# Query, value and output products from split factors in the last six blocks, and expert weights fetched by chunk

## The chip, the cores and the metric

The kernel runs on one core of one Trainium2 chip. The metric is the device time of one execution in microseconds (us). Three runs of the kernel before gave 1141.47, 1142.01 and 1142.49 us; the median is 1142.01 us.

## What is computed

The reference is one transformer layer on 4096 tokens of 512 numbers (2 sequences of 2048), all in float32. Each half of the layer adds a normalised result to its input.

```python
x = x + layernorm(attention(layernorm(x)))
x = x + layernorm(experts(layernorm(x)))

# attention: 16 heads of 32, 64 latent keys, the 4 best of them per token and head
Q = h @ Wq.T + bq;  V = h @ Wv.T + bv          # 512 x 512 each
logits = einsum('bhtd,lhd->bhtl', Q, latent) / sqrt(32)
top, idx = top_k(logits, 4)
weighted = einsum('bhtk,bhtkd->bhtd', softmax(top), latent[idx])
out = (weighted + V) @ Wo.T + bo

# experts: weights rounded to -1, 0, 1 times one scale per matrix; 2048 hidden
hidden = silu(h @ Wu.T) * (h @ Wg.T)
out = hidden @ Wd.T
```

## The kernel before, in words

**Tiling.** The 4096 tokens are cut into 8 blocks of 512 (`NB = 8`, `TB = 512`), and a block into 4 tiles of 128 tokens (`TT = 4`). The 2048 hidden columns of the experts are cut into 16 chunks of 128 (`EC = 16`). The main loop (L1020) goes over blocks b and, inside, over chunks e. While the experts of block b run, the attention of block b+1 is worked in between, and the first normalisation of block b+2 too. A prologue (the list `FIRST_STEPS`) does the attention of block 0, the queries of block 1, and the rounding of the expert weights. So the loop of block 0 carries the attention of block 1 (without queries), the loops of blocks 1 to 6 carry the attentions of blocks 2 to 7 in full, and the loop of block 7 carries none.

**Order of work.** The order is written out by hand: each engine (TensorE, VectorE, ScalarE, GpSimd, and SyncE's queue, which issues all DMAs) takes its instructions in the order in which the Python code emits them. In a chunk e this order is:

```python
F.up("u", e); do(3); F.tanh(e); do(0); F.silu(e)
F.up("g", e); do(1); F.gate(e); F.high(e)
F.down(e - 1); do(2); F.low(e)
```

`do(k)` emits whatever `pieces` (L937) has put at place (e, k) by `put(e, k, f, ...)`: the steps of the attention. `up("u")` is 8 matmuls into the PSUM bank "u", `up("g")` 8 into the bank "g", `down(e - 1)` 8 into the four banks "acc". Each of the banks "u" and "g" is there once, so `up("u", e + 1)` waits until `silu(e)` on VectorE has read "u", and `up("g", e + 1)` until `gate(e)` on VectorE has read "g". `down(e)` needs `low(e)`, the last thing that VectorE does in chunk e. Two more banks, "at", are shared by all steps of the attention.

**Types.** Expert matmuls work on float32r operands, one pass each; the hidden numbers and the normalised input are given as a high and a low part (`hi`, `lo`; `hT_f`, `lT_f`), which makes two matmuls of each. The products of the attention (`q` L349, `v` L435, `y_pe` L455, `o` L464, `l` L361) are plain float32 matmuls; the trace shows each as two matmul instructions.

**Steps of the attention.** `q(c)` is a quarter of the queries, with its bias added on ScalarE; `l(c)` the logits of four heads, as two tiles w(2c), w(2c+1) that ScalarE copies out. For each of the eight tiles w(i): `m` (eight best), `r` (mark the four best, subtract the largest), `e` (exponentials on ScalarE), `n` (normalise), `z` (transpose and send through DRAM to a transposed tile wT). Tile i has `m` in chunk i+1, `r` in chunk i+1 at place 2, `e` in chunk i+2 at place 3, ahead of `tanh`, and `n` and `z` in chunk i+2. `v(c)` and `y_pe(c)` add V and the weighted latent vectors in one bank, `o(t)` is the output product of a tile of tokens, `o_bias` adds bo on VectorE. The normalisations, the residual sums on GpSimd and the transposes for the next experts (`f_blocks`, `f_load`, `f_split`, through DRAM) follow in chunks 11 to 15. `a_stats`, `a_apply`, `a_blocks` in chunks 9 and 10 prepare block b+2, and `a_load` brings its transposed input hT at the end of chunk 15. The result of the experts is normalised by `y_stats` (chunk 0 of the next block) and `y_out` (chunk 1), which frees the four "acc" banks.

**Memory.** All rounded expert weights stay on chip in 24 buffers of 128 x 1024 (tag "chunk"), wq, wv and wo in float32 beside them.

Of the kernel before, what the change touches and what calls it, by code (L numbers as in the profile page):

```python
# [17 lines left out]
P = 128  # L18
# [11 lines left out]
TAKEN = -3.2e38  # L30

# [15 lines left out]
"""  # L47

# [10 lines left out]
def latent_attention_ternary_glu(  # L59
# [43 lines left out]

    def acc_psum(name):
        return ps_acc.tile([P, D], F32, tag="acc", name=name)

    def transposed(which, b, name, dtype):  # L110
        return work.tile([P, DC, TB], dtype, tag=f"{which}{b % 2}", name=name, bufs=1)
# [10 lines left out]
    late = work.tile([P, DC, D], F32, tag="xa", name="raw_d_6", bufs=1)  # L122
    for n, i in RAW_ORDER:
        raw[n, i] = wpool.tile([P, CH], F32, tag="chunk", name=f"raw_{n}_{i}", bufs=6 * DC)
    for q in range(DC):
        raw["d", 6 + q] = late[:, q, :]
# [13 lines left out]
    def load_normed(b):  # L140
        normed[b] = work.tile([P, TT, D], F32, tag="xa", name=f"xa_{b}", bufs=1)
        nc.sync.dma_start(
            out=normed[b], in_=x_in[b * TB : (b + 1) * TB, :].rearrange("(t p) d -> p t d", p=P)
        )
# [9 lines left out]
    wq = wpool.tile([P, DC, D], F32, name="wq")  # L154
    wv = wpool.tile([P, DC, D], F32, name="wv")
    wo = wpool.tile([P, DC, D], F32, name="wo")
# [75 lines left out]
    def sign(n, i):  # L232
        j = i if n != "d" or i < 6 else 6 + (i - 6) // 2
        if (n, j) not in tern:
            tern[n, j] = wpool.tile([P, CH], F32R, tag="chunk", name=f"tern_{n}_{j}", bufs=6 * DC)
        q = tern[n, j] if j == i and i < 6 or n != "d" else tern[n, j][:, (i % 2) * D : (i % 2 + 1) * D]
        nc.scalar.activation(q, raw[n, i], AF.Sign, bias=minus_magic)

# [52 lines left out]
    class Attention:  # L291
# [15 lines left out]
        def a_stats(self, t):  # L307
            self.norm_a.stats(t, normed[self.b][:, t, :])
# [4 lines left out]
        def a_apply(self, t):  # L313
            self.norm_a.apply(normed[self.b][:, t, :], normed[self.b][:, t, :], t)
# [14 lines left out]
        def a_blocks(self, t):  # L329
            self.blocks("a", t, normed[self.b][:, t, :])  # L330

        def a_load(self):
            self.hT = transposed("X", self.b, f"hT_{self.b}", F32)
# [101 lines left out]
        def v(self, c, psum=at_psum):  # L435
            if self.attnT is None:
                self.attnT = transposed("Y", self.b, f"attnT_{self.b}", F32)
# [74 lines left out]
        def f_load(self, half):  # L512
            if half == 0:
                self.whole = work.tile([P, 4, TB], F32, tag="xa", name=f"hw_{self.b}", bufs=1)
# [7 lines left out]
        def f_split(self, t):  # L522
            if t == 0:
                self.hi = transposed("X", self.b, f"hT_f{self.b}", F32R)
                self.lo = transposed("Y", self.b, f"lT_f{self.b}", F32R)
# [11 lines left out]

    class FirstAttention(Attention):  # L540
# [19 lines left out]
        def a_trans_pe(self, t):  # L560
            if self.hT is None:
                self.hT = transposed("X", self.b, f"hT_{self.b}", F32)
# [53 lines left out]
        def v_pe(self, c):  # L616
            if self.attnT is None:
                self.attnT = transposed("Y", self.b, f"attnT_{self.b}", F32)
# [68 lines left out]
        def f_high(self, t):  # L687
            if not hasattr(self, "hi"):
                self.hi = transposed("X", self.b, f"hT_f{self.b}", F32R)
            nc.scalar.copy(self.hi[:, :, t * P : (t + 1) * P], self.pt[t])  # L690

        def f_low(self, t):
            if not hasattr(self, "lo"):
                self.lo = transposed("Y", self.b, f"lT_f{self.b}", F32R)
# [7 lines left out]
    class Experts:  # L702
# [6 lines left out]
        def up(self, n, e):  # L709
# [5 lines left out]
            for k, i in pairs:  # L715
                nc.tensor.matmul(  # L716
                    p, lhsT=tern[n, 2 * k + e // 8][:, (e % 8) * P : (e % 8 + 1) * P],
# [3 lines left out]


# [29 lines left out]
        def down(self, e, tiles=range(TT), last=True):  # L752
            if e == 0:
                self.acc = [acc_psum(f"acc_{self.b}_{t}") for t in range(TT)]
            wd = tern["d", e // 2][:, (e % 2) * D : (e % 2 + 1) * D]
# [46 lines left out]
        def y_out(self, t, engine=nc.gpsimd):  # L802
# [4 lines left out]
            else:  # L807
                y = row(f"y_{self.b}_{t}")
                self.norm.apply(y, self.acc[t], t)
# [29 lines left out]
    def query_place(c):  # L839
        if c < 3:  # L840
            if not hasattr(nxt, "early"):
                nxt.early = transposed("Y", 1, "qT_1", F32)
# [94 lines left out]
    def pieces(A, after):  # L937
# [6 lines left out]
        if A.b > 1:  # L944
# [12 lines left out]
        for c in range(2):  # L957
            if A.b > 1:
                put(4 + 2 * c, 0, A.v, c, gate_psum)
                put(4 + 2 * c, 0, A.y, c)  # L960
            put(4 + 2 * c, 0, A.l, c + 2)
            if A.b == 1:

                put(4 + 2 * c, 2 - c, A.v, c)
                put(4 + 2 * c, 2 - c, A.y, c)
        for c in range(2, DC):
            put(4 + 2 * c, 1, A.v, c)
            put(4 + 2 * c, 1, A.y, c)
# [15 lines left out]
        put(10, 2, A.o, 0, range(DC), gate_psum)  # L984
        put(10, 2, A.o_bias, 0)
        for t in range(1, TT):
# [4 lines left out]
            put(10, 2, A.o, t)  # L991
# [174 lines left out]
```

## Time and profile before

| what | value |
|---|---|
| profiled execution, span from first to last instruction | 1140.3 us |
| the three timed runs, median | 1142.01 us, 1.7 us above the span |
| TensorE busy | 1127.9 us of the span (99%), granted clock 0.998 |
| VectorE, ScalarE, GpSimd busy | 836.3, 411.9, 163.5 us |
| one middle block, 499.0 to 637.5 us | 138.5 us: TensorE 138.4, VectorE 104.7, ScalarE 43.5, GpSimd 17.3 us busy |
| DMA in the same stretch | 28% of 16 engines, 84 GB/s |

A matmul's own duration in the profile contains its way through the array; what counts for throughput is the distance between starts. "PE" is a matmul, "PEld" its load of weights, which overlaps other matmuls. "DVE" is VectorE, "ACT" ScalarE, "POOL" GpSimd, "SP" SyncE's queue. L716 is `up`, L759 `down`, L353 `q`, L440 `v`, L457 `y_pe`, L468 `o`, L367 `l`.

### The profile page before, as it was taken

To read this page: it belongs to the slowest core of one execution; us is meant where nothing else is said; L and a number is where in the kernel's file an instruction comes from. 1 tells how busy PE (TensorE), PEld (TensorE's weight loads), DVE (VectorE), ACT (ScalarE), POOL (GpSimd) and SP (SyncE) were. 2 spreads that over 40 slices of the span, in tenths; PEclk is the share of its full clock that TensorE was granted. 3 is DMA by queue.
4 is the path that set the end of the run, shared out by engine and by line. 5 is a ranking of instruction groups with operands and counts; after the bars stand their busy time and mean duration, and the time that the engine had idled before them with its cause. 6 is when DMAs were issued, how large, how long until landed. Compare 5 with 4: busy or idle time off the path is not lost.

```text
span 1140.3 us, 14487 instructions
## 1 busy us (share of the span) xinstructions
PE 1127.9 (99%) x4602; PEld 771.9 (68%) x4602; DVE 836.3 (73%) x2952; ACT 411.9 (36%) x714; POOL 163.5 (14%) x203
## 2 busy tenths in 40 slices
PE   9999999999999999999999999999999999999997
PEld 5547666767667675776657766586675866758886
DVE  6978968687866887678877778678786787847435
ACT  4985642332233332333214333153321433224223
POOL 1057003110032000320002200022001120021200
PEclk9999999999999999999999999999999999999999
DMA  9800221432213322222222222232321412102000
GB/s 350 305 0 20 74 93 38 111 120 84 82 52 98 102 86 81 72 77 93 93 74 75 83 93 95 63 99 66 112 75 56 111 65 93 61 5 74 37 1 37
DMA packets 98428, 97.16 MB, mean 85 GB/s; under 512 B 8368, under 2 KB 70832, under 8 KB 98352
## 3 DMA queue, kind: packets, MB, share of 16 engines
q1 hardware_dynamic: 98352, 96.24, 26.8%
q8 instruction: 36, 0.59, 0.2%
q14 instruction: 40, 0.33, 0.1%
HBM read 59.51 MB, written 36.70 MB: 84 GB/s over the span
## 4 chain that ended last, share of the span: by engine, by line
PE 89%; DVE 5%; DMA 4%; ACT 1%; issue 0%; SPq 0%; ACTq 0%; DVEq 0%
PE pg L716 20%; PE pu L716 19%; PE acc L759 19%; PE po L468 8%; PE pv L440 8%; PE pq L353 7%; PE pv L457 2%; PE pl L367 2%; DMA raw_d<-in_wdT 1%; DVE left L393 1%; DMA raw_g<-in_wgT 1%; DMA wv<-in_wvT 1%; DVE m L385 1%; DMA raw_u<-in_wuT 1%; PE pq L577 1%; DMA hT<-far_a 1%
## 5 line engine op out<-in xcount | busy, mean ns | idle before, releaser
L716 PE MATMUL pg<-hT_f,tern_g 128*128 128x512 f32 x512 | 207.8, 406 | 0.0
L716 PE MATMUL pu<-hT_f,tern_u 128*128 128x512 f32 x512 | 204.8, 401 | 0.0
L759 PE MATMUL acc<-tern_d,hi 128*128 128x512 f32 x512 | 203.6, 398 | 0.0
L759 PE MATMUL acc<-tern_d,lo 128*128 128x512 f32 x512 | 200.0, 391 | 1.0 <-DVE lo L749 0.9
L716 PE MATMUL pg<-lT_f,tern_g 128*128 128x512 f32 x512 | 199.8, 390 | 0.0
L716 PE MATMUL pu<-lT_f,tern_u 128*128 128x512 f32 x512 | 199.1, 390 | 0.0
L725 ACT ACTIVATE h<-pu,columns 128x512 f32<-128x512 f32 x128 | 87.1, 680 | 202.8 <-PE pu L716 202.8
L728 DVE SCALAR_TENSOR_TENSOR h<-h,pu 128x512 f32<-128x512 f32 x128 | 85.9, 671 | 93.5 <-ACT h L725 93.5
L744 ACT CAST hi<-h 128x512 fp32r<-128x512 f32 x128 | 79.1, 618 | 199.2 <-DVE h L733 199.1
L733 DVE TENSOR_TENSOR h<-h,pg 128x512 f32<-128x512 f32 x128 | 86.5, 675 | 63.4 <-PE pg L716 62.3
L759 PEld LDWEIGHTS acc<-tern_d,hi 128*128 128x128 f32 x512 | 96.2, 188 | 32.8 <-issue 13.6
L716 PEld LDWEIGHTS pg<-hT_f,tern_g 128*128 128x128 f32 x512 | 96.2, 188 | 25.3 <-issue 1.4
L716 PEld LDWEIGHTS pu<-hT_f,tern_u 128*128 128x128 f32 x512 | 96.1, 188 | 25.1 <-issue 3.1
L759 PEld LDWEIGHTS acc<-tern_d,lo 128*128 128x128 f32 x512 | 96.2, 188 | 22.9 <-DVE lo L749 2.2
L716 PEld LDWEIGHTS pu<-lT_f,tern_u 128*128 128x128 f32 x512 | 96.2, 188 | 22.5 <-issue 3.1
L716 PEld LDWEIGHTS pg<-lT_f,tern_g 128*128 128x128 f32 x512 | 96.3, 188 | 21.5 <-issue 2.9
L749 DVE TENSOR_TENSOR lo<-h,hi 128x512 fp32r<-128x512 f32 x128 | 89.9, 702 | 23.1 <-ACT hi L744 23.1
L440 PE MATMUL pv<-hT,wv 128*128 128x512 f32 x224 | 100.8, 593 | 0.3 <-ACT w L375 0.3
L393 DVE MATCH_REPLACE8 left<-m,w 128x64 f32<-128x64 f32 x512 | 100.3, 209 | 0.0
L468 PE MATMUL po<-wo,attnT 128*128 128x512 f32 x224 | 97.3, 592 | 0.0
L353 PE MATMUL pq<-hT,wq 128*128 128x512 f32 x192 | 86.7, 595 | 0.9 <-DMA hT<-far_a 0.6
L468 PEld LDWEIGHTS po<-wo,attnT 128*128 128x128 f32 x224 | 42.6, 190 | 50.7 <-issue 48.3
(140 smaller groups left out, 1312.0 us busy)
## 6 DMA issues: line engine op xcount, KB each, us to landing
dz<-z SPq DMA_DIRECT2D x56, 256.0 KB, 2.0
wT<-dz SPq DMA_DIRECT2D x224, 64.0 KB, 1.9
x<-in_x SPq DMA_DIRECT2D x32, 256.0 KB, 3.7
out_x<-x SPq DMA_DIRECT2D x32, 256.0 KB, 2.0
far_f<-zf SPq DMA_DIRECT2D x28, 256.0 KB, 2.8
hw<-far_f SPq DMA_DIRECT2D x56, 128.0 KB, 3.5
xa<-in_x SPq DMA_DIRECT2D x6, 1024.0 KB, 5.3
far_a<-za SPq DMA_DIRECT2D x24, 256.0 KB, 2.9
```

The costliest lines, as they stand in the source:

```text
L353: nc.tensor.matmul(pq, lhsT=wq[:, k, c * P : (c + 1) * P], rhs=self.taken(k), start=(k == 0), stop=(k == DC - 1),)
L367: nc.tensor.matmul(pls[pr][:, t * P : (t + 1) * P], lhsT=qT[rows, t * P : (t + 1) * P], rhs=lk[rows, c, :], start=True, stop=True, tile_po ...
L393: nc.vector.match_replace(left[:, g, :], m8[:, g, :], w[:, g, :], TAKEN)
L440: nc.tensor.matmul(self.pv[c], lhsT=wv[:, k, c * P : (c + 1) * P], rhs=self.ordered(k), start=(k == 0), stop=False,)
L468: nc.tensor.matmul(self.po[t], lhsT=self.attnT[:, c, t * P : (t + 1) * P], rhs=wo[:, c, :], start=(c == 0), stop=(c == DC - 1),)
L716: nc.tensor.matmul(p, lhsT=tern[n, 2 * k + e // 8][:, (e % 8) * P : (e % 8 + 1) * P], rhs=self.parts[i][:, k], start=(k, i) == pairs[0], s ...
L725: nc.scalar.activation(self.h[e], self.pu[e], AF.Tanh, scale=half_u[0])
L728: nc.vector.scalar_tensor_tensor(self.h[e], self.h[e], 1.0, self.pu.pop(e), ALU.add, ALU.mult)
L733: nc.vector.tensor_tensor(self.h[e], self.h[e], self.pg.pop(e), ALU.mult)
L744: nc.scalar.copy(hi, self.h[e])
L749: nc.vector.tensor_tensor(lo, self.h.pop(e), self.hid[e][0].bitcast(F32), ALU.subtract)
L759: nc.tensor.matmul(self.acc[t], lhsT=part[:, t * P : (t + 1) * P], rhs=wd, start=(e == 0 and i == 0), stop=(e == EC - 1 and i == 1),)
```

## The change

In the loops of blocks 1 to 6 (the attentions of blocks 2 to 7) the products q, v and o are no longer four-by-four float32 matmuls. Each factor is split into a high part (times `CUT`, rounded to float32r) and the rest, and from these a third, combined tile is formed. One product becomes three float32r matmuls: 4 into a "cross" bank and 8 into a "high" bank, and the two banks are joined by ScalarE (cross plus bias) and VectorE (high times 1 + 2^-12, plus that).

- `SplitAttention` replaces `Attention` for blocks 2 to 7. Its input is split by `x_high` (ScalarE), `x_low` and `x_difference` (VectorE), two instructions of 128 x 1024 each; `v_split` splits the sum of V and the weighted vectors (two on ScalarE, one on VectorE, one on GpSimd for each c). `a_load` moves from chunk 15 to chunk 12.
- A `q` or a `v` takes two banks: both "at" banks. `o` takes "u" and "g" for tiles 0 and 2, both "at" banks for tiles 1 and 3. The addition of bo moves from VectorE to GpSimd.
- `v` moves from chunks 4, 6, 8, 10 to chunks 5, 7, 8 and the end of 9.
- In `r` the subtraction of the largest from w leaves VectorE; a small instruction (`least`) takes its place, and `e` becomes eight exponentials of 64 columns with that as bias instead of one of 512.
- `y_out` applies the normalisation on ScalarE (`apply_scalar`) instead of VectorE.
- wq, wv and wo are split once (`parts`, in the loops of blocks 0 and 1) into 18 of the 24 "chunk" buffers. So the rounded expert weights are written to DRAM during block 0 (`keep`), and from block 1 on each chunk's weights are fetched two chunks ahead (`fetch_up`, 512 KB a chunk; `fetch_down`, 512 KB every second chunk), through SyncE's queue.

```diff
+    def part_high(n, w, j):
+        h = unit(f"{n}_high_{j}", F32R)
+        nc.scalar.activation(h, w[:, 2 * j : 2 * j + 2, :], AF.Copy, scale=CUT)
...
+    def part_rest(n, w, j):
...
+        nc.vector.tensor_tensor(src, src, h.bitcast(F32), ALU.subtract)
+        low = unit(f"{n}_low_{j}", F32R)
+        nc.scalar.activation(low, src, AF.Copy, scale=1.0 / STEP)
...
+    class SplitAttention(Attention):
...
+        def x_high(self, j):
...
+            nc.scalar.activation(
+                self.piece("h", j), self.piece("d", j).bitcast(F32), AF.Copy, scale=CUT
+            )
+        def x_low(self, j):
...
+            nc.vector.tensor_tensor(
+                self.piece("l", j), self.piece("d", j).bitcast(F32),
+                self.piece("h", j).bitcast(F32), ALU.subtract,
+            )
+        def x_difference(self, j):
+            nc.vector.scalar_tensor_tensor(
+                self.piece("d", j), self.piece("h", j).bitcast(F32), -STEP,
+                self.piece("l", j).bitcast(F32), ALU.mult, ALU.add,
+            )
...
+        def products(self, n, c, high, cross, moving):
+            cols = slice(c * P, (c + 1) * P)
+            for k in range(DC):
+                nc.tensor.matmul(
+                    cross, lhsT=form(n, "d", k)[:, cols], rhs=moving("d", k),
+                    start=(k == 0), stop=(k == DC - 1 and n == "q"),
+                )
+            for i, which in enumerate("hl"):
+                for k in range(DC):
+                    nc.tensor.matmul(
+                        high, lhsT=form(n, which, k)[:, cols], rhs=moving(which, k),
+                        start=(i == 0 and k == 0), stop=(i == 1 and k == DC - 1),
+                    )
+        def joined(self, dst, high, cross, bias):
+            nc.scalar.activation(dst, cross, AF.Identity, bias=bias)
+            nc.vector.scalar_tensor_tensor(dst, high, 1.0 + STEP, dst, ALU.mult, ALU.add)
...
+        def v_split(self, c):
...
+            nc.scalar.activation(h, self.sum, AF.Copy, scale=CUT)
+            nc.scalar.activation(d, self.sum, AF.Copy, scale=CUT * STEP)
+            nc.vector.tensor_tensor(l, self.sum, h.bitcast(F32), ALU.subtract)
+            nc.gpsimd.tensor_tensor(d, l.bitcast(F32), d.bitcast(F32), ALU.subtract)
+        def o(self, t, high, cross):
+            toks = slice(t * P, (t + 1) * P)
+            order = [("d", k) for k in range(DC)] + [(w, k) for w in "hl" for k in range(DC)]
+            if t == 0:
+                order = [(w, k) for w in "hld" for k in range(DC - 1)]
+                order += [(w, DC - 1) for w in "hld"]
...
+        def o_bias(self, t):
...
+            nc.scalar.copy(o, cross)
+            nc.gpsimd.tensor_tensor(o, o, bo_sb, ALU.add)
+            nc.vector.scalar_tensor_tensor(o, high, 1.0 + STEP, o, ALU.mult, ALU.add)
...
+        def e(self, i):
+            nc.scalar.activation(self.top[i], self.top[i], AF.Exp)
+            for g in range(G):
+                nc.scalar.activation(
+                    self.w[i][:, g, :], self.w[i][:, g, :], AF.Exp, bias=self.least[:, g, :]
+                )
...
-                self.norm.apply(y, self.acc[t], t)
+                self.norm.shift(t)
+                self.norm.apply_scalar(y, self.acc[t], t)
...
+        if split:
+            for c, e in enumerate((5, 7, 8)):
+                put(e, 1, A.v, c)
+                put(e, 1, A.y_pe, c)
+                put(e, 2, A.v_join, c)
+                put(e + 1, 0, A.v_split, c)
+            put(9, 2, A.v, 3)
+            put(10, 1, A.y_pe, 3)
+            put(10, 1, A.v_join, 3)
+            put(10, 1, A.v_split, 3)
...
+            put(12, 0, after.a_load)
+            late = after.b == 2
+            for j in range(2):
+                put(15 if late else 13, 2, after.x_high, j)
+            for j in range(2):
+                put(15 if late else 14, 2 if late else 0, after.x_low, j)
+            for j in range(2):
+                put(15, 2, after.x_difference, j)
...
+        i = b * EC + e + 2
+        if EC <= i < NB * EC:
+            fetch_up(i)
+        if e % 2 and EC <= i - 1 < NB * EC:
+            fetch_down(*divmod((i - 1) // 2, EC // 2))
+    def parts(b, e):
+        for n, w, at_b, at_e in (("q", wq, 0, 8), ("v", wv, 0, 11), ("o", wo, 1, 0)):
+            if b == at_b and 0 <= e - at_e < 2:
+                part_high(n, w, e - at_e)
+                part_rest(n, w, e - at_e)
+                part_difference(n, e - at_e)
```

## The prediction

> **What bounds the kernel now.** I read the page's busy table and chain first, then the chain in order of time for one middle block, then the timeline of all engines.
>
> ```profile
> PE 1127.9 (99%) x4602; PEld 771.9 (68%) x4602; DVE 836.3 (73%) x2952; ACT 411.9 (36%) x714; POOL 163.5 (14%) x203
> ...
> PE 89%; DVE 5%; DMA 4%; ACT 1%; issue 0%; SPq 0%; ACTq 0%; DVEq 0%
> ```
>
> TensorE has almost no gap, and the chain that ends last is TensorE for 89%. The chain in order of time (start, length) gives the price of each group:
>
> ```profile
> 504.75 3.44 PE pq L353 x8
> 508.18 1.82 PE acc L759 x8
> ...
> 558.75 1.81 PE pg L716 x8
> ...
> 588.03 13.73 PE po L468 x32
> ```
>
> A float32 instruction costs 0.43 us (3.44 / 8), a float32r one 0.227 (1.81 / 8). But VectorE is close behind. In the first block, where no q stands between the chunks, the timeline shows it as the bound already:
>
> ```profile
> 108.59 0.68 DVE L749 TENSOR_TENSOR lo<-h,hi 128x512 fp32r<-128x512 f32 x1
> ...
> 109.33 0.50 PE L759 MATMUL acc<-tern_d,lo 128*128 128x512 f32 x1 [0.41 <-DVE lo L749]
> ...
> 116.25 0.68 DVE L749 TENSOR_TENSOR lo<-h,hi 128x512 fp32r<-128x512 f32 x1
> ...
> 116.99 0.50 PE L759 MATMUL acc<-tern_d,lo 128*128 128x512 f32 x1 [0.45 <-DVE lo L749]
> ```
>
> From `lo` to `lo` VectorE needs 7.66 us a chunk there, and TensorE waits for it. What fills them shows in chunk 8 of a middle block:
>
> ```profile
> 565.72 0.18 DVE L397 TENSOR_TENSOR top<-m 128x32 f32<-128x32 f32 x1
> 565.82 0.68 DVE L749 TENSOR_TENSOR lo<-h,hi 128x512 fp32r<-128x512 f32 x1
> 566.00 0.23 ACT L402 ACTIVATE top<-top 128x32 f32<-128x32 f32 x1 [1.82 <-DVE top L397]
> 566.13 0.61 ACT L403 ACTIVATE w<-w 128x512 f32<-128x512 f32 x1
> 566.42 1.10 DVE L385 MAX8 m<-w 128x8 f32<-128x64 f32 x8
> 566.65 0.67 ACT L725 ACTIVATE h<-pu,columns 128x512 f32<-128x512 f32 x1
> ...
> 567.60 0.65 DVE L728 SCALAR_TENSOR_TENSOR h<-h,pu 128x512 f32<-128x512 f32 x1
> 568.17 0.18 DVE L408 TENSOR_REDUCE ri<-top 128x8 f32<-128x32 f32 x1
> ...
> 570.54 0.65 DVE L733 TENSOR_TENSOR h<-h,pg 128x512 f32<-128x512 f32 x1
> ```
>
> Call T the end of `lo` (566.50). The order is a loop through two engines: `r` ends, ScalarE does `e` and then `tanh` (ends T+0.82), VectorE does `m` (to T+1.10), `silu` (0.57), `n` and `z` (2.37), `gate` (0.57), the marks of `r` (1.67), its subtraction (0.60), `top` (0.11), `lo` (0.68): 7.67 in all. `lo` has slack before TensorE needs it: it ends at 510.70, and `down` begins at 514.79.
>
> **What the change removes.** Each (c, k) product goes from 2 x 0.43 to 3 x 0.227 us, 0.185 less. 48 products in a block make 8.9 us, six blocks 53 us. All of it is on the path, as long as nothing else sets it. The FP8 and Floating Point Precision page of the Trainium skill (TensorE Precision Notes) counts float32 as four passes; three of four would save a quarter, 10.4 us a block at 0.864 us a product, where the rows give 8.9; the rows decide.
>
> **What it adds, through one middle block** (t = 0 at the end of the last `down` of the block before; before: 495.53). I follow the emitted order with the rows' durations.
>
> *Chunks 0 and 1.* `q(0)` now has a join on VectorE, queued ahead of `y_stats`: it starts when the query ends (2.95) and `y_stats` run 3.6 to 6.8 instead of from about -1. GpSimd's rsqrt (2.07, 636.66 to 638.73) ends at 9.0. The four normalisations on ScalarE (spacing 0.71) end at 10.0 to 12.1; `down(0)` wants the four banks at 10.4 to 11.7 and waits 0.4. Behind them on ScalarE stands the bias of `q(1)` (to 12.75), behind that on VectorE its join (13.4), `m` (14.6), `gate` (15.2), `r`, `lo` (17.75). `down(1)` wants that `lo` at 17.5: the slack of 4.1 us is gone.
>
> *Chunks 2 to 8*, from `lo` to `lo`. Eight exponentials take the place of one: a row of 32 columns moves on after 0.13 us (566.00 to 566.13), and 32 columns more are 32 x 0.81 ns (0.615 for 512 against 0.227 for 32), so 0.16 to 0.17 each, 1.34 for eight where one cost 0.52. `tanh` ends at T+1.64, so `silu` starts at 1.67 and not 1.10. `least` (0.13, between the 0.09 of a memset and the 0.20 of a reciprocal) replaces the subtraction. A plain chunk: 1.67 + 0.57 + 2.37 + 0.57 + 1.67 + 0.13 + 0.11 + 0.68 = 7.8 (chunks 2, 4). With a query (3, 5) its bias waits on ScalarE for `tanh` (to 2.3), the join follows on VectorE (to 2.95), then `m`: 10.2, and 10.8 with the join of `v(0)` in 5. A split V (6, 8) puts ScalarE's split and VectorE's difference ahead of `silu`: 9.5 in 6 (two copies of w come first), 9.0 in 8 with a join, 8.4 in 7. Sum 63.5.
>
> *To chunk 10.* `z(7)` ends 5.2 after `lo(8)`; its way through DRAM is the next price (SyncE's timeline, and a line of the list of DMA issues with the time to landing):
>
> ```profile
> 578.20 0.34 SPq L425 DMA_DIRECT2D dz<-z  x1
> 580.28 1.73 SPq L428 DMA_DIRECT2D wT<-dz  x4
> ...
> wT<-dz SPq DMA_DIRECT2D x224, 64.0 KB, 1.9
> ```
>
> The last issue starts at 581.6 and lands 1.9 later: 5.4 us after `z`. Then `y_pe(3)` takes 1.15. So `down(9)` starts at 17.75 + 63.5 + 5.2 + 5.4 + 1.15 = 93.0. Before it was 90.4 (585.92), and TensorE alone would now be there at 84.1 (eight quarters of q and v less, 5.9, and the wait of 0.4 for hT gone): 8.9 of waits in place of 6.3 of gain.
>
> *Chunk 10.* `gate(10)` frees the bank "g" for `o(0)`, and VectorE reaches it only after the join and the difference of `v(3)` (2.95 after `down(9)` starts, because they need `y_pe(3)`) and four `a_apply` (1.92): 5.45, where `o(0)` wants it at 3.2. With 0.3 more for a bank, `o(3)` ends 15.05 after `down(9)` starts; before 15.5; without waits 12.7.
>
> *Chunk 11 to the next block.* 27.4 before. GpSimd's addition of bo (1.3 us) lies between ScalarE and VectorE in each `o`, `low(10)` comes 0.4 late; GpSimd's residual sums start 5.5 after `o(3)` instead of 3.8 (605.16 against 601.4), half of which chunk 12 takes up, so the transposed input of the experts comes 1 us later, just in time: 27.9. Chunk 0 adds 0.15 for `lo(15)` behind `x_difference` (5.6 for 5.45).
>
> Block: 93.0 + 15.05 + 27.9 + 5.6 = 141.6 against 90.4 + 15.5 + 27.4 + 5.45 = 138.75: **2.8 us longer**, times four. The loop of block 6 has no `a_apply`: +0.9. Block 1 has the parts of wo in chunks 0 and 1, two halves of 1.35 us on VectorE ahead of `lo`: +5.5. At the end of block 0 three splits of hT stand in one place: ScalarE 2.3, then VectorE 1.3 + 2.6 ahead of `lo(15)`, which `down(15)` awaits: +3.3. Sum 11.4 + 0.9 + 5.5 + 3.3 = 21. On the profiled 1140.3 that is 1161; the median stands 1.7 above the span: **1163 us**.
>
> **What costs nothing, and its cover.** The fetches are 12.6 MB a block, some 89 GB/s on top of 84, at a DMA share of 28%; they lead by two chunks (over 12 us), a 1024 KB load lands in 5.3 us. In SyncE's queue each takes about 0.4 us of issue; up_0 of the next block stands behind eight hw issues (3.6 us) and lands about 1 us before it is used: that cover is thin. The writes of block 0 wait for `sign` in a chunk already past. `v`'s GpSimd differences (1.3 each) have a chunk of time, except the last, which lies under the wait for `gate(10)`.
>
> **Bounds.** Eight exponentials: 8 x 0.13 = 1.0 (nothing for the extra columns) to 8 x 0.253 = 2.0 (no overlap); I take 1.34 because neighbouring rows overlap by 0.09. In seven chunks and six blocks: -13 to +28 us. DRAM way of wT: 5.4, up to 3.2 more (longest wait for dz 3.6, longest landing 3.2): 0 to +19. A float32 operation slowed by GpSimd (one `lo` takes 0.94 at 608.57): 0 to +6. Waits that I count and that overlap: down to half of the 12 us of waits a block, -36. The ScalarE: Activation LUTs page of the skill (Rules for kernel authors) budgets 0.3 us per instruction plus 0.83 ns an element, 2.8 us for eight; the sum by it would be about 1225. The rows of 0.13 to 0.52 between starts speak against it.
>
> **Rivals.** *A, TensorE stays the bound:* the queues have more room than I count. All covered is 1142 - 53 = 1089; half of the waits is about 1127. For it: 99% busy now, VectorE 73%. Against: the loop of 7.66 us that already stops TensorE in block 0. It decides where a block's loop falls by over 2.8 us, that is, below 138.75. *B, ScalarE's small exponentials don't overlap:* +28, 1191. *C, weights or wT come late:* wherever a fetch stands ahead, +3 to 4 us a block, 1185; against it the low DMA share. *D, the change doesn't do what it says:* a permuted moving operand in one pass costs 0.43: 144 x 0.43 against 41.5 a block, +20 each, 1285. Against: the permuted pq row (595 ns) equals the plain po row (592).
>
> **Chances.** Forecast (1150 to 1178) 0.46, A 0.23, B 0.20, C 0.09, D 0.02. A measurement tells 0.2% (2.3 us) from nothing: faster 0.22 (A but for its edge), the same 0.03, slower 0.75. The range leaves out the better half of A and the end of B with C and D: 1112 to 1203; the forecast's own range is 1150 to 1178.
>
> **What would show it.** Right: pq, pv, po groups of 12 at 0.227; pu, pg waiting for DVE h and pv for ACT and DVE in chunks 3 to 6; VectorE from `lo` to `lo` over 10 us where a query joins; po waiting 2 us for `gate`; eight ACT rows of about 0.25 with 0.17 between starts. Wrong: TensorE at 99% again with blocks of 130 us; an ACT row for 64 columns spaced at 0.25 (B); waits for DMA up_ or wT (C).

## The result, and the profile after

| | before | changed |
|---|---|---|
| median | 1141.86 us (4 runs, 1141.47 to 1142.49) | 1240.49 us (4 runs, 1234.78 to 1242.33) |
| ratio | 1 | 1.0853, 95% interval 1.0828 to 1.0878 |
| span of the profiled execution | 1140.3 us | 1240.5 us |
| mean granted clock of TensorE in it | 0.998 | 0.975 |

The changed kernel is 8.5% slower: 98.6 us, where the prediction had 21. From the page of the changed kernel, the busy table and the chain that ended last, by engine and by line:

```profile
PE 1139.7 (92%) x4890; PEld 836.3 (67%) x4890; DVE 887.0 (71%) x3054; ACT 553.4 (45%) x1170; POOL 242.4 (20%) x257
...
DVE 31%; PE 27%; DMA 18%; ACT 14%; POOL 4%; issue 3%; SPq 3%; ACTq 0%; DVEq 0%; POOLq 0%
PE acc L972 7%; PE pu L923 6%; PE pg L923 5%; DMA dz<-z 5%; ACT w L742 4%; DVE left L730 4%; DVE h L945 3%; DVE h L940 2%; DVE z L497 2%; DVE w L490 2%; DMA far_f<-zf 2%; PE pv L534 2%; DMA wT<-dz 2%; DVE w L487 2%; DMA hT<-far_a 2%
```

TensorE's part of the chain has fallen from 89% to 27%. In its place come VectorE and ScalarE, which was foreseen, and 18% of transfers, which the forecast had put at nothing: `dz`, `far_f`, `wT` and `hT` are small transfers of the attention, not the fetched weights themselves.

Where the time went shows when the ends of VectorE's `lo` (L961) are read from the timeline, chunk by chunk. Each number below is the step from the `lo` of one chunk to the next (us); "next 0" belongs to the following block. The last four lines are experiments told further down (experiments 1, 3, 4 and 13).

```
chunk               1    2    3    4    5    6    7    8    9   10   11   12   13   14   15  next 0
block 0
before            7.5  8.0  7.7  7.7  8.2  8.2  9.2  7.7  6.3 24.4  5.3  5.7  4.1  6.1  4.5  7.1
changed           7.5  8.0  7.7  7.8  8.2  8.2  9.2 11.7 10.6 21.2  7.6  9.6  4.0  8.3 10.0 12.4
mean of blocks 2 to 5
before           12.1  8.5  8.4 11.2  8.9 11.2  7.7  7.7  6.8 23.1  5.5  5.7  4.1  6.5  4.2  7.1
changed          10.0  8.1 10.5  8.2 11.1 10.2  9.0 10.7 11.2 24.2  5.3  5.7  4.1  8.9  6.0  9.7
one_fetch        10.0  8.1 10.5  8.2 11.1 10.2  8.7  9.8  9.1 23.9  5.3  5.7  4.1  7.2  5.3 10.0
one_fetch_one_exp 10.6 7.7  9.7  7.7 10.4  9.8  8.3  9.4  7.7 23.6  5.3  5.7  4.1  7.2  5.3 10.1
fetch_alone      17.2  8.5  8.4 11.2  8.9 11.2  7.7  7.7  6.8 23.1  5.5  5.7  4.2  8.9  3.8  6.5
three_terms_best 11.0  7.9  7.8  7.7  9.7  9.1  8.8  8.5  8.0 21.9  5.5  5.7  4.1  7.4  4.0  6.6
```

By block, from `lo` of chunk 0 to the next: block 0 takes 152.0 us (127.7 before), block 1 154.3 (138.4), blocks 2 to 5 149.8, 153.4, 154.9 and 153.4 (138.4 to 138.7), block 6 139.2 (136.0); what follows is the same (78.9, 79.2). So a quarter of the loss lies in block 0, and in the middle blocks it lies in chunks 8, 9, 14, 15 and the next 0, with 1 us in chunk 10, while chunks 1 to 7 together are no slower than before.

The chain in order of time, in chunks 6 to 8 of a middle block of the changed kernel (start, length, what), shows steps that the chain of before did not have, transfers between the chunks (`z` goes to DRAM as `dz` and comes back as `wT`):

```profile
760.48 0.03 DVE top L735
760.51 5.76 DMA dz<-z
...
766.36 0.71 DVE z L497
767.07 0.57 DVE h L945
...
769.12 5.44 DMA dz<-z
...
775.94 1.96 DMA wT<-dz
...
778.03 1.94 PE pv L534 x2
779.97 3.71 PE acc L972 x8
```

Before, `dz` landed 2.0 us after its issue in the median; here it takes 5.8 and 5.4. SyncE's timeline of the same stretch says why:

```profile
768.11 0.43 SPq L282 DMA_DIRECT2D up<-up_store  x1
768.64 0.39 SPq L289 DMA_DIRECT2D down<-down_store  x1
769.12 0.38 SPq L502 DMA_DIRECT2D dz<-z  x1
774.62 1.75 SPq L505 DMA_DIRECT2D wT<-dz  x4
776.41 0.43 SPq L282 DMA_DIRECT2D up<-up_store  x1
776.94 0.38 SPq L502 DMA_DIRECT2D dz<-z  x1
781.14 1.74 SPq L505 DMA_DIRECT2D wT<-dz  x4
```

The 256 KB of `dz` are issued on the same queue half a microsecond behind 1024 KB of weights. SyncE then waits for `dz` before it may issue `wT`, and only after that the next fetch, which so again falls just ahead of the next `dz`: the lateness keeps itself up. VectorE suffers too (its `z` at 766.36 waits for a buffer that the late `dz` holds), and TensorE waits 3.6 us at 778.03 for the `wT` of the sixth tile, w(5).

TensorE's timeline right behind that wait (an instruction of `acc` takes 0.227 us from start to start elsewhere) holds the second thing that no step of the prediction had:

```profile
780.50 0.63 PE L972 MATMUL acc<-down,lo 128*128 128x512 f32 x1
780.92 0.63 PE L972 MATMUL acc<-down,hi 128*128 128x512 f32 x1
781.35 0.63 PE L972 MATMUL acc<-down,lo 128*128 128x512 f32 x1
...
783.81 0.39 PE L923 MATMUL pu<-lT_f,up 128*128 128x512 f32 x1
784.03 0.39 PE L923 MATMUL pu<-hT_f,up 128*128 128x512 f32 x1
```

After the wait the same instructions start 0.43 us apart until 783.5, and 0.227 apart again from then on. The granted clock shows it too. In the view of windows (stretch, its length, TensorE busy and its instructions, granted clock, DMA share, GB/s) the clock is 0.50 up to 783.5 and 0.96 behind:

```profile
780.00:783.50 3.50, 3.50 (x9) 0.50 0.27 87
783.50:786.00 2.50, 2.50 (x12) 0.96 0.85 245
```

The eight `acc` so take 3.71 us in the chain and not 1.81: the wait costs its own length and 1.9 us more.

### The profile page after: what moved, and what is told of

It reads as the page before. It is cut to its first block, busy times and chain, and to the rows that moved or that the text cites. A ratio compares the mean times of both kernels' runs of the same rounds, so it can differ in the third digit from the quotient of the medians.

```text
span 1240.5 us, 16293 instructions
## 1 busy us (share of the span) xinstructions
PE 1139.7 (92%) x4890; PEld 836.3 (67%) x4890; DVE 887.0 (71%) x3054; ACT 553.4 (45%) x1170; POOL 242.4 (20%) x257
## 4 chain that ended last, share of the span: by engine, by line
DVE 31%; PE 27%; DMA 18%; ACT 14%; POOL 4%; issue 3%; SPq 3%; ACTq 0%; DVEq 0%; POOLq 0%
PE acc L972 7%; PE pu L923 6%; PE pg L923 5%; DMA dz<-z 5%; ACT w L742 4%; DVE left L730 4%; DVE h L945 3%; DVE h L940 2%; DVE z L497 2%; DVE w L490 2%; DMA far_f<-zf 2%; PE pv L534 2%; DMA wT<-dz 2%; DVE w L487 2%; DMA hT<-far_a 2%
## 5 line engine op out<-in xcount | busy, mean ns | idle before, releaser
L923 PE MATMUL pu<-hT_f,up 128*128 128x512 f32 x448 | 178.7, 399 | 21.5 <-DVE h L940 19.5
L923 PE MATMUL pg<-hT_f,up 128*128 128x512 f32 x448 | 178.3, 398 | 8.3 <-DVE h L945 8.3
L972 PE MATMUL acc<-down,lo 128*128 128x512 f32 x448 | 179.0, 400 | 6.3 <-DVE lo L961 6.2
L972 PE MATMUL acc<-down,hi 128*128 128x512 f32 x448 | 182.4, 407 | 0.9 <-ACT y L348 0.9
L923 PE MATMUL pu<-lT_f,up 128*128 128x512 f32 x448 | 176.9, 395 | 0.2 <-DVE lT_f L609 0.2
L923 PE MATMUL pg<-lT_f,up 128*128 128x512 f32 x448 | 174.6, 390 | 0.0
L923 PEld LDWEIGHTS pu<-hT_f,up 128*128 128x128 f32 x448 | 85.0, 190 | 48.8 <-DVE h L940 28.2
L972 PEld LDWEIGHTS acc<-down,hi 128*128 128x128 f32 x448 | 85.9, 192 | 44.8 <-issue 21.9
L923 PEld LDWEIGHTS pg<-hT_f,up 128*128 128x128 f32 x448 | 84.1, 188 | 31.1 <-DVE h L945 10.8
L972 PEld LDWEIGHTS acc<-down,lo 128*128 128x128 f32 x448 | 86.2, 192 | 27.0 <-DVE lo L961 10.6
L961 DVE TENSOR_TENSOR lo<-h,hi 128x512 fp32r<-128x512 f32 x128 | 91.1, 712 | 18.3 <-ACT hi L956 18.3
L742 ACT ACTIVATE w<-w,least 128x64 f32<-128x64 f32 x384 | 96.4, 334 | 0.1
```

The source lines that it names most:

```text
L742: nc.scalar.activation(self.w[i][:, g, :], self.w[i][:, g, :], AF.Exp, bias=self.least[:, g, :])
L923: nc.tensor.matmul(p, lhsT=self.weight(n, k, e), rhs=self.parts[i][:, k], start=(k, i) == pairs[0], stop=(k, i) == pairs[-1],)
L961: nc.vector.tensor_tensor(lo, self.h.pop(e), self.hid[e][0].bitcast(F32), ALU.subtract)
L972: nc.tensor.matmul(self.acc[t], lhsT=part[:, t * P : (t + 1) * P], rhs=wd, start=(e == 0 and i == 0), stop=(e == EC - 1 and i == 1),)
```

## The experiments

Ratios are to the kernel before, with their 95% intervals.

**1. One fetch a block.** In `fetch_up` and `fetch_down`:

```
         b, e = divmod(i, EC)
+        if e > 0:
+            up_part[b, e] = up_part[b, 0]
+            return
```

> Each block fetches the weights of one chunk and uses them for all sixteen (so the products of the other chunks are taken with the wrong weights), which cuts the fetched bytes from 12.6 MB to about 1 MB a block; all else as in the changed kernel. Theory Q (the transfers that stand ahead in the DMA rings make dz, far_f and the first up late: dz lands 5 us after its issue where it took 2.0): about 1170, dz back at 2.0 us, blocks near 143 us. Theory E (the eight exponentials, 2.7 us where I took 1.34, are the loss): at least 1215, blocks still over 150 us.

1210.3 us (1.0599, 1.0583 to 1.0615): 30 us less, below the 1215 of E and above the 1170 of Q. `dz` is back at 2.0 us, chunks 9, 8 and 14 lose 2.1, 0.9 and 1.7 us, and blocks 2 to 5 take 146 to 149 us. So the fetches cost 30 us here (the writes of block 0 are still in), and they are not all.

**2. One exponential.** `SplitAttention` without its own `r` and `e`, so that it takes those of `Attention`, one exponential on ScalarE and the subtraction on VectorE:

```
-        def r(self, i):
...
-        def e(self, i):
-            nc.scalar.activation(self.top[i], self.top[i], AF.Exp)
-            for g in range(G):
-                nc.scalar.activation(
-                    self.w[i][:, g, :], self.w[i][:, g, :], AF.Exp, bias=self.least[:, g, :]
-                )
```

> The changed kernel with the subtraction on VectorE and one exponential of 512 columns, as before the change. Theory Q: about 1225, since the loop then waits for dz just as long. Theory E: about 1180, 1.3 to 2.1 us less in each of eight chunks and six blocks, less the subtraction of 0.6.

1225.6 us (1.0732, 1.0700 to 1.0763): 15 us less, as theory Q had it, and `dz` still late (4.2 us in the median). The row of the eight on ScalarE in the changed kernel, with the instruction ahead and the one behind:

```profile
749.82 0.23 ACT L740 ACTIVATE top<-top 128x32 f32<-128x32 f32 x1 [0.58 <-DVE top L735]
749.95 2.00 ACT L742 ACTIVATE w<-w,least 128x64 f32<-128x64 f32 x8
751.86 0.67 ACT L937 ACTIVATE h<-pu,columns 128x512 f32<-128x512 f32 x1
```

`tanh` starts 1.91 us after the first exponential: 0.24 for each, where I had taken 0.167 and 1.34. The page ScalarE: Activation LUTs of the Trainium skill (What ACT_TABLE_LOAD costs) gives 280 ns plus 0.833 ns an element for an instruction whose bias is a column of its own, and an overlap of 93 ns with the next: 0.333 and 0.240 for 64 columns. The trace agrees with both (334 ns in the mean of the 384 rows, 0.24 apart). I had read only that page's rough rule, and then set it aside.

**3. Both edits.**

> Both of these edits together (products of fifteen chunks with the wrong weights again). If each cause stands alone in its own chunks the gains add up: about 1150 by either theory. If they hide one another, more than the sum of the two gains: 1120 to 1140.

1181.8 us (1.0347, 1.0328 to 1.0366): 58.7 less, 14 more than the two gains added, though both expected times were too low by 30 us and more. Each hid part of the other in chunks 8 and 9: 10.7 and 11.2 become 9.4 and 7.7 only when both are gone.

**4. The fetch alone**, added to the kernel before, with `keep`, `fetch_up`, `fetch_down`, `MOVES` and `weights` as in the change:

```
-                    p, lhsT=tern[n, 2 * k + e // 8][:, (e % 8) * P : (e % 8 + 1) * P],
+                    p, lhsT=self.weight(n, k, e),
...
-            wd = tern["d", e // 2][:, (e % 2) * D : (e % 2 + 1) * D]
+            wd = down_part[self.b, e // 2] if self.b > 0 else tern["d", e // 2]
```

> The kernel before, with its float32 products, whose weights are written out in block 0 and fetched by chunk as in the changed kernel; nothing else changed. Theory Q: slower than before by 5 to 10 us a block, 1175 to 1200. Theory E: 1142 to 1150, the fetches are hidden.

1182.7 us (1.0361, 1.0344 to 1.0378): 41 us, with no split at all. Here the fetches fall between the `dz` (2.3 us), and chunks 2 to 9 keep their times to 0.1. The loss is in other places, chunk 14 (+2.4, `far_f` and `hw`) and chunk 1 (+5.1). TensorE's timeline of chunk 1 in one block (the kernel before waits there 0.6 us in all its blocks together):

```profile
513.92 6.59 PE L383 MATMUL pq<-hT,wq 128*128 128x512 f32 x8 [3.60 <-DMA hT<-far_a]
525.36 3.60 PE L383 MATMUL pq<-hT,wq 128*128 128x512 f32 x8
```

The first query waits 3.6 us for the transposed input, which now stands behind eight `hw` and three fetches, and then costs 6.59 us at the lower rate in place of 3.6. (The changed kernel loads this input three chunks earlier and does not pay this.) Block 0 also shows what the writes cost: it is 2.4 us longer, 0.9 in chunk 8 and 1.4 in chunk 9, before the first fetch is issued in chunk 14; the `dz` at 155.21 there stands behind two writes of 512 KB.

**5. The fetches on ScalarE's queue**, in `fetch_up` and `fetch_down` of the changed kernel:

```
-        nc.sync.dma_start(
+        nc.scalar.dma_start(
             out=part.bitcast(F32).rearrange("p (n k c) -> p n k c", n=2, c=P), in_=up_store[e]
```

> The changed kernel with all fetches of weights issued by ScalarE on its own DMA queue; the loads and stores of the attention stay on SyncE's. Theory Q1 (dz waits in order behind the fetch on the same queue): dz lands in 2 to 3 us again, 1212 to 1225. Theory Q2 (the 16 engines are shared, whatever the queue): dz stays near 4 to 5 us, 1235 to 1250, the more so if each issue holds ScalarE for the 0.4 us that SyncE's rows show.

1227.2 us (1.0757, 1.0730 to 1.0784): 13 less. From the lists of DMA issues (KB, median us from issue to landing), the changed kernel and then this one:

```profile
up<-up_store SPq DMA_DIRECT2D x112, 512.0 KB, 5.0
...
dz<-z SPq DMA_DIRECT2D x56, 256.0 KB, 3.8
...
far_f<-zf SPq DMA_DIRECT2D x28, 256.0 KB, 3.1
```

```profile
up<-up_store ACTq DMA_DIRECT2D x112, 512.0 KB, 3.8
...
dz<-z SPq DMA_DIRECT2D x56, 256.0 KB, 2.3
...
far_f<-zf SPq DMA_DIRECT2D x28, 256.0 KB, 6.2
```

With a queue of its own the fetch no longer stands ahead of `dz`: Q1 is right for `dz` (its time of 1212 to 1225 is missed by 2), and chunk 9 falls by 2.2 us. But `far_f`, a transfer of the same size, now takes twice as long, and the step to chunk 14 rises from 8.9 to 9.6. So the order in the queue is one part of the price and the traffic itself another. The page DMA: Bandwidth & Descriptors of the skill (Issuing engines are not separate DMA queues) says that a second issuing engine saves only the sequencer's time; these rows show that it also takes 1.5 us off one small transfer and adds 3.1 to another.

**6. Another place for the parts**, behind `lo`, and for the splits of block 2's input:

```
-            late = after.b == 2
+            late = False
...
-            parts(b, e)
             if e == 0 and b == NB - 1:
                 F.low(e)
...
                 F.low(e)
+            parts(b, e)
```

> The changed kernel with the splits of wq, wv and wo put behind lo on VectorE in their chunks, and with the splits of block 2's input in chunks 13 and 14 as in the other blocks. Blocks 0 and 1 are 24.3 and 15.9 us longer than before; the chunks 8, 9, 11, 12, 15 and the next 0 that hold these operations have +4.0, +4.3, +2.3, +3.9, +5.5 and +5.3. If the operations stand in the way of lo only by their place: 10 to 16 us less, 1225 to 1230. If VectorE and ScalarE have no room for them there: under 4 us less.

1235.9 us (1.0829, 1.0798 to 1.0860): 4.6 less, within the spread of the runs. Block 0 gets 4.1 us shorter and block 1 4.5 longer (158.7). The steps that shrink (8, 11, 15) are paid in 10, 13 and 14. So moving these operations only moved the loss.

**7. No parts but the high ones**, on top of experiment 3:

```
-        return parted[n, which][k // 2][:, (k % 2) * D : (k % 2 + 1) * D]
+        return parted[n, "h"][k // 2][:, (k % 2) * D : (k % 2 + 1) * D]
...
-                part_rest(n, w, e - at_e)
-                part_difference(n, e - at_e)
```

> The kernel with one fetch a block and one exponential (1181.8), in which the high parts of wq, wv and wo also stand in for the low parts and the differences, so that VectorE's 1.23, ScalarE's second 1.06 and GpSimd's 2.39 of each half go (wrong products); ScalarE's first 1.04 stays. Theory P (these operations, which I gave no price in block 0, make it 20 us longer than before): block 0 falls by 8 to 13 us and block 1 by 4 to 6, 1164 to 1170. If block 0 is long because of the late splits of block 2's input alone: under 5 less.

1170.6 us (1.0253, 1.0237 to 1.0268): 11.1 less than experiment 3. Block 0 falls from 147.9 to 139.4, as theory P had it, and block 1 from 145.0 to 142.8, half of what it had. The timeline of the changed kernel shows how one half lies in the way, in chunk 8 of block 0:

```profile
159.09 1.04 ACT L295 ACTIVATE q_high<-wq 128x1024 fp32r<-128x1024 f32 x1
160.17 1.23 DVE L301 TENSOR_TENSOR wq<-wq,q_high 128x1024 f32<-128x1024 f32 x1 [2.82 <-ACT q_high L295]
161.31 0.69 DVE L961 TENSOR_TENSOR lo<-h,hi 128x512 fp32r<-128x512 f32 x1
161.43 1.06 ACT L303 ACTIVATE q_low<-wq 128x1024 fp32r<-128x1024 f32 x1 [1.29 <-DVE wq L301]
```

VectorE stands idle for 2.8 us, because the high part comes behind two `sign` on ScalarE; `lo` is queued behind the subtraction, and `tanh` of the next chunk behind the low part. That makes the 4.0 us of that step.

**8. No joins**, the changed kernel with

```
-            nc.vector.scalar_tensor_tensor(dst, high, 1.0 + STEP, dst, ALU.mult, ALU.add)
...
-            nc.vector.scalar_tensor_tensor(o, high, 1.0 + STEP, o, ALU.mult, ALU.add)
```

> The changed kernel without the twelve joins of a block on VectorE (the high products are computed but not added, so queries, values and outputs lack their main part); second banks, ScalarE's copies, differences, GpSimd's work, fetches and eight exponentials stay. Theory J (the joins, 0.69 each, are what three_terms took off VectorE's loop): 12 x 0.69 = 8.3 us a block, most of it on the path, 1195 to 1205. Theory K (it was the rest of what three_terms leaves out: two banks in o, GpSimd's operations beside VectorE's, 2.4 us of differences): 1220 to 1235.

1195.5 us (1.0478, 1.0459 to 1.0497): 45 less, as theory J had it. Twelve operations of 0.69 in six blocks are 50 us, and the kernel without them is faster by nine tenths of that.

**9. Three terms in one bank.** High x high, low x high and high x low, added up by TensorE; the core of the edit:

```
-                nc.tensor.matmul(
-                    cross, lhsT=form(n, "d", k)[:, cols], rhs=moving("d", k),
...
+            terms = [(w, x, k) for w, x in ("hh", "lh", "hl") for k in range(DC)]
+            for w, x, k in terms:
+                nc.tensor.matmul(
+                    bank, lhsT=form(n, w, k)[:, cols], rhs=moving(x, k),
+                    start=((w, x, k) == terms[0]), stop=((w, x, k) == terms[-1] and n == "q"),
+                )
...
-            nc.gpsimd.tensor_tensor(d, l.bitcast(F32), d.bitcast(F32), ALU.subtract)
+            nc.scalar.activation(h, pv, AF.Identity, bias=bias)
+            nc.vector.scalar_tensor_tensor(l, pv, bias, h.bitcast(F32), ALU.add, ALU.subtract)
```

> The three products are high x high, low x high and high x low (the product of the two low parts, some 2^-24 of the whole, is left out), all accumulated in one PSUM bank; so no join, no difference operand and no second bank, with the same number of one-pass products, the same fetches and the same eight exponentials. Theory V (VectorE's loop with the joins is the bound in chunks 2 to 8): 12 joins of 0.69 and 2.4 of differences go in each block, half or more on the path: 1190 to 1210. If the fetches alone set the blocks: 1225 to 1240.

1175.8 us (1.0301, 1.0286 to 1.0317): 65 less with the same number of products, the same fetches and exponentials, and more than theory V had (1190 to 1210). 45 of them are the joins by experiment 8. Two VectorE operations for the difference of the input, 2.4 us a block, are gone as well, and so are operations that GpSimd did beside VectorE. Two VectorE rows, the same operations on the same shapes, from the lists of groups by form (busy us, mean ns), first of the changed kernel and then of this one:

```profile
L487 DVE SCALAR_TENSOR_TENSOR w<-left,w 128x512 f32<-128x512 f32 x64 | 50.3, 786 | 0.0
...
L353 DVE TENSOR_SCALAR xa<-xa,mv_a,rs_a 128x512 f32<-128x512 f32 x24 | 16.3, 731 | 0.0
```

```profile
L478 DVE SCALAR_TENSOR_TENSOR w<-left,w 128x512 f32<-128x512 f32 x64 | 41.0, 640 | 0.0
L344 DVE TENSOR_SCALAR xa<-xa,mv_a,rs_a 128x512 f32<-128x512 f32 x24 | 11.6, 539 | 0.0
```

14 us of VectorE's time in these two groups are gone with GpSimd's operations.

**10. The same, lighter**: experiments 2, 6 and 9 together.

> The kernel with three terms, one exponential of 512 columns with the subtraction on VectorE, and the splits of blocks 0 and 1 placed behind lo. If the costs add: three_terms less 15 to 25 for the exponentials and 10 to 16 for the places, 1155 to 1180. If the fetches were the bound by themselves: as slow as fetch_alone or slower, 1183 and more.

1175.3 us (1.0305, 1.0281 to 1.0329): a miss. The time lies in the expected range by luck, because experiment 9 came out lower than expected; the gain over it, put at 25 to 41 us, is 0.5. Without the joins neither the exponentials nor the places give anything. The slow steps are chunks 7 to 9 (10.8, 11.7 and 9.9), where TensorE waits for the late `wT`.

**11. Three terms with one fetch.**

> The kernel with three terms (no joins), fetching the weights of one chunk per block and using them for all sixteen (wrong weights in the others). Without joins the full fetch gave 1175.8; with joins, one fetch took 30 off. If the fetches cost the same whether VectorE has the joins or not: about 1146. If the joins are what turns a late dz into lost time (no slack left): 1160 to 1170. If the loops had been hiding part of the fetches: under 1140.

1121.8 us (0.9821, 0.9806 to 0.9836): 54 less than with the full fetch, more than the 30 of experiment 1. So the joins' loop had been covering part of the fetches, the last of the three cases. Its busy table and chain:

```profile
PE 1089.8 (98%) x4890; PEld 824.0 (74%) x4890; DVE 837.2 (75%) x2994; ACT 508.9 (46%) x1092; POOL 164.9 (15%) x203
...
PE 80%; DVE 12%; ACT 3%; DMA 3%; issue 1%; SPq 0%; POOL 0%; ACTq 0%; DVEq 0%
```

TensorE is the bound again, and blocks 2 to 5 take 133.3 us where they took 138.6 before: the saving of the products is real, 5 of the 8.9 us a block come through.

**12. A fetch that stays out of the way.** Three terms; all down weights but the first pair of chunks and the up and gate weights of chunks 0 and 1 stay on the core, then also the fetches of up and gate weights on ScalarE's queue, then also one exponential:

```
+        if e < 2 and b > 1:
+            up_part[b, e] = up_part[1, e]
+            return
...
-            wd = down_part[self.b, e // 2] if self.b > 0 else tern["d", e // 2]
+            wd = down_part[self.b, 0] if self.b > 0 and e < 2 else tern["d", e // 2]
...
-        if e % 2 and EC <= i - 1 < NB * EC:
+        if e == EC - 1 and b < NB - 1:
```

> The kernel with three terms, which keeps the down weights (but the first two chunks') and the up and gate weights of chunks 0 and 1 on the core and fetches the rest, 7.9 MB in place of 12.6 MB a block, none in chunks 14 and 15 beside the loads of the transposed input but one. Theory Q: the step to chunk 14 falls from 8.9 to about 6.5 us and dz lands in about 3: 1150 to 1160. If the bytes don't matter but any fetch ahead of dz does: 1165 to 1172.

> The same with the fetches of up and gate weights issued on ScalarE's queue. Theory Q1 (order in the queue): dz lands in 2.0 to 2.3 us, pv waits for wT under 8 us in all (26 with three terms): 1135 to 1148. If ScalarE's issues cost as much as they give: as the run before.

> The same with one exponential of 512 columns and the subtraction on VectorE. If the eight exponentials still lie in the loop: 5 to 15 less. If TensorE sets the chunks by now: within 3 of the run before.

1137.7 us (0.9951, 0.9935 to 0.9968), 1130.4 (0.9900, 0.9883 to 0.9916) and 1124.5 (0.9841, 0.9813 to 0.9870). The first is better than I expected: 38 us for 37% fewer fetched bytes, with the step to chunk 14 down from 8.9 to 7.1, though `dz` is only back to 3.8 us where I had about 3. The bytes are fewer and also stand elsewhere; no run separates the two. The queue gives 7 more (`dz` at 2.3 us), the single exponential 6.

**13. The best version**: the last of these with the low parts of the weights, and those of block 2's input, on GpSimd:

```
-        nc.vector.tensor_tensor(low, src, parted[n, "h"][j].bitcast(F32), ALU.subtract)
+        nc.gpsimd.tensor_tensor(low, src, parted[n, "h"][j].bitcast(F32), ALU.subtract)
...
-            nc.vector.tensor_tensor(
+            (nc.gpsimd if self.b == 2 else nc.vector).tensor_tensor(
                 self.piece("l", j), self.piece("l", j).bitcast(F32),
```

> The kernel with three terms, resident down weights, fetches on ScalarE's queue and one exponential (1124.5), with the low parts of wq, wv and wo, and those of block 2's input, computed on GpSimd in place of VectorE. If VectorE's order is what they cost in blocks 0 and 1 (14 us more than before in block 0): 6 to 12 less, 1112 to 1119. If GpSimd's 2.4 us come too late for the first products, or slow VectorE beside them: 1122 or more.

1120.0 us (0.9807, 0.9792 to 0.9822): 1.9% faster than the kernel before and 9.7% faster than the changed one, with the whole computation in it but the low x low products. The step itself gave 4.5, less than the 6 to 12 expected, and its interval overlaps that of the kernel ahead of it. In the traces block 0 falls from 141.8 to 136.0, and block 1 gives 2.6 of it back. Block 0 is still 8.3 us longer than in the kernel before.

## Why the prediction was wrong, step by step

**The saving** held. Twelve one-pass products of a value take 2.84 us in the chain of the changed kernel, 0.236 each, so rival D is out:

```profile
789.18 0.95 PE pv L660 x4
790.13 1.89 PE pvh L666 x8
```

And experiment 11 shows the kernel faster than before as soon as nothing else sets the chunks.

**The walk through a middle block** can be set beside the trace stage by stage (changed: the block from 695.6 to 850.6; one fetch: from 533.5 to 680.5; a stage ends with its last row, 0.4 later for `o` than the prediction counted):

| stage | before | forecast | changed | one fetch |
|---|---|---|---|---|
| t0 to `lo(1)` | 15.0 | 17.75 | 17.4 | 17.4 |
| `lo(1)` to `lo(8)` | 63.5 | 63.5 | 68.9 | 66.6 |
| `lo(8)` to `down(9)` | 11.8 | 11.75 | 15.4 | 12.8 |
| `down(9)` to the end of `o(3)` | 15.8 | 15.05 | 17.9 | 17.5 |
| to the next t0 | 32.6 | 33.5 | 35.2 | 32.7 |
| block | 138.7 | 141.6 | 154.9 | 147.0 |

- *Chunks 0 and 1*: right, the slack of `lo(1)` is gone and no more.
- *Chunks 2 to 8*: the mechanism was right (VectorE and ScalarE from `lo` to `lo`, 10.5 and 11.1 us where a query joins, forecast 10.2 and 10.8). The term "1.34 for eight" was mis-sized: 1.91. Seven chunks of the difference are 4.0 us, and one fetch lies 3.1 over the forecast, so other terms of these chunks were too high by 0.9.
- *z(7) to down(9)*: the 5.4 us from `z(7)` to its `wT` held (5.3 to 6.2 in the six blocks). What failed is that the walk priced this way for the last tile alone. Behind a fetch the `wT` of w(5) lands 9.8 to 10.8 us after its `z`, where it took 5.3 to 5.5, and TensorE, which needs it for the third quarter of V, waits in chunk 8 of each of the six blocks, 2.0 to 3.6 us, 16 in all. The walk has no wait there. From 778.03 TensorE then works without a gap until `down(9)` starts at 797.5: the longer stage is this wait and the lower rate behind it. With one fetch the wait stands in chunk 10, as forecast (1.7 to 1.9 us). The bound of 0 to +19 was named for z(7), and I put its value at 0.
- *Chunk 10*: the wait for `gate(10)` came in the five blocks that have `a_apply`, 3.0 us where I had 2.25. The four `a_apply` took 2.85 us beside GpSimd's `attn_d` in place of 1.92:

```profile
800.34 2.85 DVE L353 TENSOR_SCALAR xa<-xa,mv_a,rs_a 128x512 f32<-128x512 f32 x4
800.57 1.43 POOL L699 TENSOR_TENSOR attn_d<-attn_l,attn_d 128x512 fp32r<-128x512 f32 x1 [3.77 <-DVE attn_l L698]
803.12 0.67 DVE L945 TENSOR_TENSOR h<-h,pg 128x512 f32<-128x512 f32 x1
...
803.94 1.42 PE L712 MATMUL poc<-o_diff,attn_d 128*128 128x512 f32 x3 [3.02 <-DVE h L945]
```

  The ten products after the wait take 3.95 us in this block and not 2.27, again at the lower rate; these 1.7 us and the longer wait are the stage's excess.
- *Chunk 11 to the next block*: close without the full fetch (32.7 for 33.5), 1.7 us short with it: eight `hw` wait for a `far_f` that lands in 6.6 us, and "up_0 of the next block stands behind eight hw issues" came true, a wait of 1.1 us where I had written 1 us of cover.

**"What costs nothing, and its cover"** is the step that failed most: it put the fetches at nothing. It priced them by the share of the DMA engines and by the lead of the weights. Both were as I said (TensorE waits 2.0 us in all for the weights themselves), but the small transfers that share the queue had no lead. The price is 30 us in this kernel, 41 with the writes in the kernel before and 54 without joins. The writes of block 0, put at nothing too, cost 2.3 us in experiment 4.

**Block 0** was priced at +3.3 for the splits of its chunk 15 and took +24.3. With one fetch and one exponential it is still 20.2 longer than before. 8.5 of that go with the low and difference parts of wq and wv in chunks 8, 9, 11 and 12, which had no price at all. In the kernel of experiment 7, where these are gone, chunk 15 and the next 0 still take 10.0 and 10.7 us where they took 4.5 and 7.1: the splits of block 2's input stand there, and 9.1 us is nearly three times my term. Chunks 8 and 9 keep 0.7 and 1.4, about what the writes cost in experiment 4. Block 1, forecast +5.5, has 6.6 under the same two edits.

**The rivals** B and C were both named and both true, and I gave them 0.20 and 0.09 as if only one could happen. B's mechanism is right (0.24 for B's 0.25): taking the eight exponentials out gives 15 us with all fetches and 28 with one, for its 28. C's is right, with 30 for its 22. Together they make 59, since they lie in the same loop, and 1182 us remain: 40 above before, of which 20 are block 0's. So the forecast's 21, these 59 and the 17 by which block 0 missed its term make 97 of the 98.6 measured. The sum is a rough one: experiment 3 also takes out the 4 us or so that the walk had counted for the exponentials, and its block 6 came out 5 us under the forecast. The range ended at 1203 because no case had two causes at once.

Not settled: how much of the 65 us of experiment 9 beyond the joins is GpSimd beside VectorE, how much the differences on VectorE, and how much the second bank of `o`. No run separates them.

## What to carry to other kernels

A background stream that "fits" by bandwidth is priced by what it stands ahead of: list each small transfer that an engine waits for, and add the length of whatever shares its queue. Where two rivals hold at the same time, forecast and range need the case in which both do. And a product split over three cheap passes keeps its gain only if putting the parts together does not load an engine that is near the bound: accumulating all terms in one bank took 65 us off by itself, and with it fewer fetches on another queue, one exponential and the parts on GpSimd turned 8.5% slower into 1.9% faster.

## What the runs showed of the hardware

- *TensorE after an idle time.* In the changed kernel, some 50 instructions of up and down start 0.43 us apart in place of 0.227, always behind an idle time of TensorE of 1.9 to 3.6 us, and for 1 to 6 us; other idle times of 2.2 and 2.5 us had no such stretch. These alone cost TensorE some 10 us. The trace's record of the granted clock has 0.5 over them, in 13 stretches of 3.41 or 6.83 us, and all of these begin whole multiples of 3.41 us apart. So the moment of an idle time decides as well: the same wait of 3.0 us for `gate(10)` has such a stretch at it in blocks 1, 3, 4 and 5 and none in block 2. The page TensorE: Matmul & The Clock Gate of the Trainium skill (Why this matters for your kernels) warns of idle times over some 3 us; the trace shows the lower rate after shorter ones, and the trace decides. With its stretch, a wait of 3.0 us cost 4.7 (at 803.94) and one of 3.6 at least 5.5 (at 778.03).
- *VectorE beside GpSimd.* A `w` operation that takes 0.64 us took 1.11 to 1.21 in all 18 cases in which it began while `attn_d` ran on GpSimd, and ended 0.55 us after GpSimd's operation in each. At 774.28 it lasted to 775.39, 0.56 us after GpSimd's operation (773.57 to 774.83) had ended, about its own length. The page SBUF — State Buffer (SBUF: two separate sides) describes a port pair that one of the two engines holds for a whole instruction, and the trace agrees.
- *A queue's order counts.* 256 KB took 2.0 us to land with nothing ahead, 5.4 and 5.8 in the two cases shown behind weights on the same queue (1024 KB for the 5.4), and 2.3 in the median with the same bytes on another queue. It does not hold for every transfer: `far_f`, also 256 KB, went from 3.1 to 6.2 us with that change.
